# First loads in another order, seven identity products ahead of the first matmul, and later weight loads on ScalarE's queue in a two-layer gated cross-attention kernel

## The chip, the cores and the metric

The kernel runs on one core of a Trainium2 chip. Its time is device microseconds per execution, as the median of several runs. The profile comes from one profiled execution, whose own time stands beside its span below. Engines: PE is TensorE, PEld its weight loads, DVE VectorE, ACT ScalarE, POOL GpSimd, SP SyncE.

## The reference

Two gated layers work on x (8 blocks of 128 rows, 512 wide) and a context of the same shape. Cut to what matters here:

```python
x = x + tanh(g_xattn[0]) * L0_xattn(layernorm(x), ctx, mask, ...)   # 32 heads of 128
x = x + tanh(g_ffn[0])   * L0_ffn(layernorm(x), ...)                # 4-bit weights
x = x + tanh(g_xattn[1]) * L1_xattn(layernorm(x), ctx, ...)         # one head, RMS norms
x = x + tanh(g_ffn[1])   * L1_ffn(layernorm(x), ...)                # base + routed LoRA
# inside L0_xattn:
h_q = (rmsnorm(x) @ w_q.T).reshape(b, lq, 32, 128)
h_k = (ctx @ w_k.T).reshape(b, lk, 32, 128)
h_v = (ctx @ w_v.T).reshape(b, lk, 32, 128)
score = softmax(where(m, h_q·h_k + position_bias, -inf))
out = (score @ h_v) @ w_out.T
```

All of it is float32. The change touches the first stage: the keys h_k and the queries h_q of the first layer's 32 heads, worked on as 16 pairs of heads.

## The kernel before, in words

**Products.** Every float32 operand is split (`split`, lines 163 and 164) into a high part, cast by ScalarE, and a low part, the difference, by VectorE or GpSimd. A product (`product`, lines 172 to 174) is three matmuls: high by high, high by low, low by high.

**The first stage** is `keys_and_queries`. Its list `order` has 32 steps: the keys of pairs 0 to 13, the queries of pairs 0 to 15, the keys of pairs 14 and 15. The first two steps (`PLAIN = 2`) run `project_plainly`: 48 matmuls a pair, from the context blocks B11, B12, B21, B22 (named by the half of the inner dimension and the half of the tokens) and whole weights wk_h, wk_l; ScalarE copies the four results (line 541). All others run `seven`, a scheme of seven block products P1, P5, P6, P2, P7, P4, P3 in that order, 42 matmuls of 128x512 in all. Their results accumulate in PSUM: P1 in c1, P6 on top of it, then P7, then P4. Between them ScalarE copies c1 away: line 237 after P1, 244 after P6, 253 after P7, 259 after P4. TensorE can't write the next product into c1 until the copy of the one before is done; `P5`, and `P2` with the last product of the step before, lie between. VectorE then adds the other terms (lines 248, 254, 263) and SP stores the result to DRAM (line 517).

**Weights.** `load_pair` loads a pair's two weights, 256 KB each, into slots of the tag `raw`, which has six buffers that the sums `more_...` use too; the issue is line 276. A step n loads the pair of step n + 2 first. `pair_sums` makes the sums and differences of the pair of step n + 2 on VectorE (lines 294 to 296; line 306 follows later), and `pair_parts` splits them for step n + 1 (ScalarE casts line 163, low parts line 164 on VectorE, or GpSimd for P1, P2 and P4 in the key steps).

**Operands.** `context_operands` splits the four context blocks (two tiles each, the inner chunk i = 0 or 1) as `cxB..`, and makes the differences T1 to T4 (line 448) as `cxT..`. `query_operands` norms x (line 413 and 414 statistics, 400 roots on GpSimd, 419 on VectorE and 420 on ScalarE for `xq`), transposes it on TensorE by the identity (line 463, tiles `tpx`) and splits the result (469, 473, 484, 488 to 490, 494); in every third step the next part of it begins.

**What sets the order.** TensorE's order in this stage is the program's, fixed by `in_order`. On the other engines a scheduler arranges the instructions by a simulation of its own when the program is built, within their dependencies; each engine then runs its list in order. A DMA that is issued from an engine's queue stands in that engine's list, with the waits for its buffer in front of it. In the kernel before, all loads and stores are issued by SP.

Of the kernel before, what the change touches and what calls it, by code (L numbers as in the profile page):

```python
# [16 lines left out]
P = 128  # L17
NB = 8
D = 512
# [4 lines left out]
HALF = NB // 2  # L24
# [12 lines left out]
}  # L37
LAG = 3
OUT_LAG = 6


def pipeline(starts):
# [18 lines left out]
def kernel(  # L61
# [37 lines left out]
    nc = tc.nc  # L99
# [6 lines left out]
    def keep(shape, name, dtype=F32):  # L106
        return sb.tile(shape, dtype, tag=name, name=name)

    def slot(shape, tag, name, dtype=F32):
        return sb.tile(shape, dtype, tag=tag, name=name, bufs=TAGS[tag])  # L110

    def page(shape, name, dtype=F32R):


        return slot(shape, "page", name, dtype)

    def wide_row(tag, name, dtype=F32):
        return slot([P, D], tag, name, dtype)

    def ptile(shape, tag, name):  # L120
        return psum.tile(shape, F32, tag=tag, name=name, bufs=BANKS[tag])

    def wide(t):

        return t.bitcast(F32)
# [4 lines left out]
    def mark(name, inst):  # L130
        marks[name] = inst.ins
# [30 lines left out]
    def split(high, low, src, low_engine=None):  # L162
        mark("high", nc.scalar.copy(high, src))  # L163
        mark("low", (low_engine or nc.vector).tensor_tensor(low, src, wide(high), ALU.subtract))  # L164
# [16 lines left out]
    HK = NDC // 2  # L181
# [85 lines left out]
    def run(steps):  # L267
        for _ in steps:
            pass
# [1 line left out]

    raws = {}

    def load(key, src, shape=(P, D)):
        t = slot(list(shape), "raw", f"raw_{key}")
        nc.sync.dma_start(out=t, in_=src)
        raws[key] = t

    def load_pair(kind, p):
        if p < NP:  # L280
            w = {"wk": wk, "wq": wq}[kind]
            for h in (2 * p, 2 * p + 1):
                load(f"{kind}_{h}", w[:, h])

    LEFT = ("P1", "P5", "P6", "P2", "P7", "P4", "P3")

# [12 lines left out]
    def pair_parts(kind, p, sums, parts, by_pool=()):  # L299

        for which in LEFT:
            t = parts[which] = slot([P, 2, N], "v", f"{kind}{which}_{p}", F32R)
            with behind("copy"):
                split(t[:, 0], t[:, 1], sums[which], nc.gpsimd if which in by_pool else nc.vector)
            if which == "P2":
                nc.vector.tensor_tensor(sums["P3"], sums["P2"], sums["P6"], ALU.subtract)
            yield
# [53 lines left out]
            biases[g] = t  # L361


    load_pair("wk", 0)
    cx_raw = {}
    for half, dcs in ((0, (0, 1)), (1, (0, 1, 2, 3)), (0, (2, 3))):
        for dc in dcs:
            t = wide_row("wo", f"cxraw{half}{dc}")
            nc.sync.dma_start(out=t, in_=ctxT[:, dc, half * HALF * P : (half + 1) * HALF * P])
            cx_raw[half, dc] = t  # L370
    load_pair("wk", 1)
    lnw = wide_row("pT", "lnw")
    nc.sync.dma_start(out=lnw, in_=ln_w.partition_broadcast(P))
# [9 lines left out]

    ident = keep([P, P], "ident")
    make_identity(nc, ident)
    neghalf = keep([P, NB], "neghalf")
    nc.gpsimd.memset(neghalf, -0.5)

# [34 lines left out]
    def right_pages(name):  # L423
        return {n: page([P, 2, HK, HALF * P], f"{name}{n}") for n in RIGHT.values()}

    def context_operands():

        ops = right_pages("cx")
        ops["B12"] = page([P, 2, HK, HALF * P], "cxB12")
        blocks = {  # L430
            n: [cx_raw.pop((half, 2 * inner + i)) for i in range(HK)]
            for n, half, inner in (("B11", 0, 0), ("B12", 1, 0), ("B21", 0, 1), ("B22", 1, 1))
        }

        def put(n, i, src):
            o = ops[n]
            split(o[:, 0, i, :], o[:, 1, i, :], src, (nc.gpsimd, nc.vector)[i])

        for n, pair in blocks.items():
            for i, t in enumerate(pair):  # L440
                put(n, i, t)
        yield ops
        b11, b12, b21, b22 = blocks.values()
        for n, dst, one, two in (
            ("T1", b11, b12, b11), ("T2", b11, b22, b11), ("T3", b12, b22, b12), ("T4", b21, b21, b11)
        ):
            for i in range(HK):
                nc.vector.tensor_tensor(dst[i], one[i], two[i], ALU.subtract)
                put(n, i, dst[i])
        yield ops  # L450
# [59 lines left out]
    def project(kind, p, left, right):  # L510


        def kept(i, half):
            return slot([P, HALF * P], "kq", f"{kind}{i}{half}_{p}")

        def done(i, half, t):
            nc.sync.dma_start(out=stored[kind, p][:, 2 * i + half], in_=t)

        return seven(f"{kind[0]}{p}", left, right, kept, done)

    def project_plainly(kind, p, left, right):

        banks = {}
        for inner in range(2):
            for half in range(2):
                for i in range(2):
                    if inner == 0:
                        tag = ("mm", "av")[half]
                        banks[i, half] = ptile([P, HALF * P], tag, f"c{i}{half}_{kind[0]}{p}")
                    w, t = left[i], right[f"B{inner + 1}{half + 1}"]  # L530
                    terms = [
                        (
                            tuple(part[:, bass.ts(2 * inner + dc, P)] for part in w),
                            (t[:, 0, dc, :], t[:, 1, dc, :]),
                        )
                        for dc in range(HK)
                    ]
                    product(banks[i, half], terms, inner == 0, inner == 1)
        for (i, half), c in banks.items():
            t = slot([P, HALF * P], "kq", f"{kind}{i}{half}_{p}")  # L540
            mark("copy", nc.scalar.copy(t, c))
            nc.sync.dma_start(out=stored[kind, p][:, 2 * i + half], in_=t)
# [298 lines left out]
    def whole_pair(p):  # L841

        both = []
        for h in range(2 * p, 2 * p + 2):
            high, low = (wide_row("v", f"wk_{n}{h}", F32R) for n in "hl")
            split(high, low, raws.pop(f"wk_{h}"))
            both.append((high, low))
        return both
# [3 lines left out]
    def later():  # L852

        return behind(*(n for n in ("copy", "add") if n in marks))
# [8 lines left out]
    def sums_of(n):  # L863
        if n < len(order):
            k, q = order[n]
            return pair_sums("w" + k[0], q)
# [3 lines left out]
    def keys_and_queries():  # L870
        nonlocal left, sums, before
        for n, (kind, p) in enumerate(order):
            if n + 2 < len(order):
                k, q = order[n + 2]
                load_pair("w" + k[0], q)
            if n < PLAIN:
                if n + 1 == PLAIN:
                    following = {}
                    run(pair_parts("wk", n + 1, sums_of(n + 1), following))
                    sums = sums_of(n + 2)  # L880
                project_plainly(kind, p, left, of_context)
                left = following if n + 1 == PLAIN else whole_pair(p + 1)
                if n == 0:
                    next(making)
                continue
            following, casts = {}, iter(())
            if n + 1 < len(order):
                k, q = order[n + 1]
                casts = pair_parts("w" + k[0], q, sums, following, BY_POOL if n < BEFORE else ())
            now = project(kind, p, left, of_context if kind == "keys" else rows[-1])  # L890
            left = following

            for which in (now, now, before, now, before, now, now):
                next(which, None)
                next(casts, None)
            before = now
            sums = sums_of(n + 2)
            if n == 3:
                with later():
                    prep_mask()  # L900
            if n < BEFORE:
                rows.append(next(of_rows))
            if n in (14, 16, 18, 20):
                with later():
                    residual((n - 14) // 2)
            if n >= BEFORE - 1:
                for _ in range(2 - n % 2):
                    next(extra, None)
        run(before)

    with in_order(*ORD):
        keys_and_queries()
# [30 lines left out]
    def unit(u):  # L943
# [6 lines left out]

        n = 2 * (u - OUT_LAG)

# [322 lines left out]
    def ending():  # L1275

        outs = iter(range(2 * (NU - OUT_LAG), NP * NB))

# [20 lines left out]
    key, ffn, att, last = ([s(b) for b in range(NB)] for s in (keys, ffn0, xattn1, ffn1))  # L1299
# [80 lines left out]
```

## Time and profile before

| what | value |
|---|---|
| median of 3 runs | 959.51 us (958.08 to 962.11) |
| profiled execution | 959.39 us, span 957.6 us, mean granted clock 0.993 |
| TensorE busy | 919.2 us, 96% of the span |
| VectorE, ScalarE, GpSimd busy | 650.3, 505.9, 482.4 us |
| DMA | 175.00 MB, mean 183 GB/s |
| loads of wk and wq | 32 each, 256 KB, 3.6 and 3.9 us from issue to landing |

Busy times are sums over the engine's instructions; the span runs from the first to the last event of the profiled execution, and the rest of its time lies around the span. In a list of waits, a row gives the waiting engine and line, what released it, and the time in total, the number of times and the longest. In a timeline a row gives the start, the duration (of a run of like instructions together), the engine and line, and in brackets the idle time before it and what ended that.

### The profile page before, as it was taken

The numbers are of one execution on the slowest core, as the hardware profiler recorded it, in microseconds if no ns is written. First come the engines' busy times: TensorE is split into PE (matmuls) and PEld (weight loads), VectorE is DVE, ScalarE is ACT, GpSimd is POOL, SyncE is SP. The second block draws the span as 40 slices with busy tenths as digits, with TensorE's granted clock in tenths as the row PEclk, the third lists the DMA queues.
The fourth block names the chain that finished last, engine by engine and source line by source line (L and its number), as shares of the span: only waits on it lengthen the run. The fifth ranks groups of instructions, "written<-read, shape, count | busy, mean of one in ns | idle before, by whom it ended". The sixth has DMA issues, their size and how long they took to land.

```text
span 957.6 us, 16579 instructions
## 1 busy us (share of the span) xinstructions
PE 919.2 (96%) x5444; PEld 807.4 (84%) x5444; DVE 650.3 (68%) x1341; ACT 505.9 (53%) x1435; POOL 482.4 (50%) x524
## 2 busy tenths in 40 slices
PE   6989999999999988999999999999999999899998
PEld 4867788887888788999999999899898997778897
DVE  7777766676678835777766667575666767645686
ACT  5555555665664534454544545354454534666761
POOL 4834323112331485675847658385584852553431
PEclk9999999999999999999999999999999999999999
DMA  9544464789886677677665766566666655513001
GB/s 283 173 145 143 133 216 160 238 259 291 298 265 202 190 233 249 185 205 189 174 200 166 220 183 190 165 180 188 182 192 188 193 166 175 220 61 118 1 24 67
DMA packets 125269, 175.00 MB, mean 183 GB/s; under 512 B 17406, under 2 KB 55294, under 8 KB 124030
## 3 DMA queue, kind: packets, MB, share of 16 engines
q1 hardware_dynamic: 125182, 173.94, 58.2%
q8 instruction: 43, 0.70, 0.3%
q14 instruction: 44, 0.36, 0.2%
HBM read 109.85 MB, written 64.03 MB: 182 GB/s over the span
## 4 chain that ended last, share of the span: by engine, by line
PE 63%; DMA 14%; DVE 11%; issue 4%; POOL 3%; ACT 2%; SPq 2%; DVEq 0%; POOLq 0%; ACTq 0%
PE sc L628 5%; PE pso L174 5%; PE pso L172 5%; PE av L686 5%; PE pso L173 5%; PE c_v L172 4%; PE c_v L173 4%; PE c_v L174 4%; DMA raw_wk<-in_wk_dram 4%; DMA through<-s 4%; PE c_q L172 3%; PE c_q L174 3%; PE c_q L173 3%; DMA moved<-through 2%; PE c_k L172 2%
## 5 line engine op out<-in xcount | busy, mean ns | idle before, releaser
L643 ACT ACTIVATE s<-s,nm 128x128 f32<-128x128 f32 x256 | 99.9, 392 | 123.5 <-DVE nm L633 69.6
L651 POOL TENSOR_TENSOR s<-s,rs 128x512 f32<-128x512 f32 x64 | 66.7, 1043 | 100.0 <-DVE rs L649 64.5
L172 PE MATMUL pso<-wo_h,a 128*128 128x512 f32 x256 | 106.7, 417 | 2.0 <-DVE x L705 2.0
L705 DVE SCALAR_TENSOR_TENSOR x<-pso,tg,x 128x512 f32<-128x512 f32 x128 | 93.8, 734 | 17.6 <-PE pso L174 17.1
L174 PE MATMUL pso<-wo_h,a 128*128 128x512 f32 x256 | 101.7, 397 | 2.0 <-DVE a L688 2.0
L173 PE MATMUL pso<-wo_l,a 128*128 128x512 f32 x256 | 101.9, 398 | 0.0
L616 POOL TENSOR_TENSOR s<-mneg,bias 128x512 f32<-128x512 f32 x64 | 82.5, 1289 | 26.4 <-DMA through<-s 26.4
L172 PE MATMUL c_v<-wvP,cxT 128*128 128x256 f32 x288 | 83.3, 289 | 1.0 <-ACT v L253 0.7
L173 PE MATMUL c_v<-wvP,cxT 128*128 128x256 f32 x288 | 81.8, 284 | 0.0
L174 PE MATMUL c_v<-wvP,cxT 128*128 128x256 f32 x288 | 81.7, 284 | 0.0
L628 PE MATMUL sc<-k,q 128*128 128x128 f32 x512 | 73.4, 276 | 6.2 <-DMA k<-keys 6.2
L671 DVE STREAM_TRANSPOSE pT<-moved 128x512 f32<-128x512 f32 x64 | 45.2, 706 | 46.3 <-DMA moved<-through 46.3
L628 PEld LDWEIGHTS sc<-k,q 128*128 128x128 f32 x512 | 66.8, 192 | 8.5 <-issue 3.5
L688 DVE TENSOR_TENSOR a<-av,a 128x512 fp32r<-128x512 f32 x64 | 43.6, 681 | 44.6 <-ACT a L687 44.4
L686 PE MATMUL av<-pT,v 128*128 128x128 f32 x512 | 68.8, 276 | 5.0 <-DVE pT L671 5.0
L686 PEld LDWEIGHTS av<-pT,v 128*128 128x128 f32 x512 | 63.1, 192 | 6.8 <-DVE pT L671 5.5
L172 PE MATMUL c_v<-wvP,cxB 128*128 128x256 f32 x216 | 62.6, 290 | 0.0
L687 ACT CAST a<-av 128x512 fp32r<-128x512 f32 x64 | 37.3, 583 | 47.8 <-PE av L686 47.7
L164 POOL TENSOR_TENSOR wvP<-raw_wv,wvP 128x512 fp32r<-128x512 f32 x43 | 56.3, 1321 | 11.0 <-ACT wvP L163 11.0
L174 PE MATMUL c_v<-wvP,cxB 128*128 128x256 f32 x216 | 61.6, 285 | 0.0
L173 PE MATMUL c_v<-wvP,cxB 128*128 128x256 f32 x216 | 61.6, 285 | 0.0
L629 DVE TENSOR_TENSOR s<-sc,s 128x512 f32<-128x512 f32 x64 | 44.0, 687 | 23.9 <-PE sc L628 12.1
(276 smaller groups left out, 2801.0 us busy)
## 6 DMA issues: line engine op xcount, KB each, us to landing
keys<-keys SPq DMA_DIRECT2D x64, 256.0 KB, 3.6
queries<-queries SPq DMA_DIRECT2D x64, 256.0 KB, 4.0
q<-queries SPq DMA_DIRECT2D x64, 256.0 KB, 4.2
k<-keys SPq DMA_DIRECT2D x64, 256.0 KB, 4.6
through<-s SPq DMA_DIRECT2D x64, 256.0 KB, 3.7
moved<-through SPq DMA_DIRECT2D x256, 64.0 KB, 2.0
raw_wk<-in_wk_dram SPq DMA_DIRECT2D x32, 256.0 KB, 3.6
raw_wq<-in_wq_dram SPq DMA_DIRECT2D x32, 256.0 KB, 3.9
```

The lines of the kernel that those rows point to most:

```text
L164: mark("low", (low_engine or nc.vector).tensor_tensor(low, src, wide(high), ALU.subtract))
L172: nc.tensor.matmul(out, lhsT=lh, rhs=rh, start=first, stop=False, **more)
L173: nc.tensor.matmul(out, lhsT=lh, rhs=rl, start=False, stop=False, **more)
L174: nc.tensor.matmul(out, lhsT=ll, rhs=rh, start=False, stop=last, **more)
L616: nc.gpsimd.tensor_tensor(s, mneg[:, half], bias.unsqueeze(2).to_broadcast([P, NQ, HALF, Q32]), ALU.add)
L628: nc.tensor.matmul(ps[:, j, :], lhsT=q[:, cols], rhs=k[:, cols], start=True, stop=True)
L629: nc.vector.tensor_tensor(s, by_block(ps), s, ALU.add)
L643: e = nc.scalar.activation(one, one, AF.Exp, bias=nm[:, j : j + 1], accum_out=sm[:, j : j + 1])
L651: mark(f"norm{u}", nc.gpsimd.tensor_tensor(s, s, factors, ALU.mult))
L671: nc.vector.transpose(by_block(t), probs[u])
L686: nc.tensor.matmul(av[:, b, :], lhsT=v[:, cols], rhs=pT[:, b, :], start=True, stop=True)
L705: "x", nc.vector.scalar_tensor_tensor(xs[b], ps, factor, xs[b], ALU.mult, ALU.add, **out)
```

## The change

There are four edits.

1. The first loads on SP's queue are issued in the order wk_0, cx00, cx01, wk_1, cx10, cx11, cx02, cx03, cx12, cx13 instead of wk_0, wk_1, cx00, cx01, cx10, cx11, cx12, cx13, cx02, cx03 (the first digit is the half of the tokens, the second the inner chunk). wk_2 and wk_3 follow in both.
2. After the identity is made, TensorE multiplies it by itself seven times into a PSUM tile that nothing reads.
3. The low part of the first tile of block B11 is made by VectorE instead of GpSimd.
4. In the steps of `keys_and_queries` the weights of the pair of step n + 2 are loaded from ScalarE's queue instead of SP's: 60 loads in all.

```diff
+WARMING = 7
...
-    def load(key, src, shape=(P, D)):
+    def load(key, src, shape=(P, D), queue=nc.sync):
         t = slot(list(shape), "raw", f"raw_{key}")
-        nc.sync.dma_start(out=t, in_=src)
+        queue.dma_start(out=t, in_=src)
         raws[key] = t
 
-    def load_pair(kind, p):
+    def load_pair(kind, p, queue=nc.sync):
         if p < NP:
             w = {"wk": wk, "wq": wq}[kind]
             for h in (2 * p, 2 * p + 1):
-                load(f"{kind}_{h}", w[:, h])
+                load(f"{kind}_{h}", w[:, h], queue=queue)
...
-    load_pair("wk", 0)
     cx_raw = {}
-    for half, dcs in ((0, (0, 1)), (1, (0, 1, 2, 3)), (0, (2, 3))):
-        for dc in dcs:
-            t = wide_row("wo", f"cxraw{half}{dc}")
-            nc.sync.dma_start(out=t, in_=ctxT[:, dc, half * HALF * P : (half + 1) * HALF * P])
-            cx_raw[half, dc] = t
+    for inner in range(2):
+        for half in range(2):
+            if inner == 0:
+                load(f"wk_{half}", wk[:, half])
+            for dc in range(inner * HK, inner * HK + HK):
+                t = wide_row("wo", f"cxraw{half}{dc}")
+                nc.sync.dma_start(out=t, in_=ctxT[:, dc, half * HALF * P : (half + 1) * HALF * P])
+                cx_raw[half, dc] = t
     load_pair("wk", 1)
...
     make_identity(nc, ident)
+
+    idle = ptile([P, P], "av", "idle")
+    for _ in range(WARMING):
+        nc.tensor.matmul(idle, lhsT=ident, rhs=ident, start=True, stop=True)
...
-            split(o[:, 0, i, :], o[:, 1, i, :], src, (nc.gpsimd, nc.vector)[i])
+            by_pool = i == 0 and n != "B11"
+            split(o[:, 0, i, :], o[:, 1, i, :], src, nc.gpsimd if by_pool else nc.vector)
...
-                load_pair("w" + k[0], q)
+                load_pair("w" + k[0], q, nc.scalar)
```

TensorE's list is the same but for the seven products. ScalarE's list has the loads between its casts and copies, and the scheduler has arranged the lists of ScalarE, VectorE and GpSimd differently in the first 60 us and in a few steps near 225 us.

## The prediction

> **What bounds the kernel now.** I read the page's busy shares first, then the chain, then the waits of TensorE, then a table by stage, and last the timelines of ScalarE, VectorE and TensorE at the places that the change touches.
>
> ```profile
> PE 919.2 (96%) x5444; PEld 807.4 (84%) x5444; DVE 650.3 (68%) x1341; ACT 505.9 (53%) x1435; POOL 482.4 (50%) x524
> PE c_k L172 <- ACT cxB L163: 6.8, 1, 6.8
> PE c_k L172 <- ACT keys L244: 5.1, 3, 3.4
> PE c_q L172 <- ACT queries L237: 1.8, 1, 1.8
> PE c_k L173 <- DVE cxB L164: 1.3, 1, 1.3
> ```
>
> TensorE is busy 96% of the span and its order is written out, so only its idle time can be won. In the stage that the change touches (keys and queries, 0 to about 325 us) that is: 6.8 us before the first matmul, 0.6 and 1.3 at the start, 5.1 in three waits for a copy of keys (3.38, 0.85, 0.85) and 1.8 for a copy of queries. All but the first few are waits for ScalarE's copies, and ScalarE was late because of others.
>
> ```profile
> 10.00:15.00 5.00, 5.00 (x17) 3.96 (x16) 5.00 (x4) 4.10 (x8) 4.09 (x4) 1.00 1.06 396
> 15.00:20.00 5.00, 3.73 (x17) 2.75 (x16) 5.00 (x8) 1.27 (x3) 1.39 (x1) 1.00 1.07 285
> 20.00:25.00 5.00, 5.00 (x24) 4.14 (x23) 5.00 (x10) 3.83 (x9) 3.13 (x2) 1.00 0.90 264
> 30.00:35.00 5.00, 5.00 (x24) 4.14 (x23) 5.00 (x20) 4.30 (x10) 4.75 (x7) 1.00 0.14 54
> ```
>
> The columns after the width are busy time of TensorE, its weight loads, VectorE, ScalarE and GpSimd, the granted clock, the DMA share and GB/s. VectorE is busy 5.00 of 5.00 in every slice from 10 to 35 us: it paces the start, and the DMA engines are full from 10 to 20.
>
> ```profile
> 35.85 0.60 ACT L237 COPY keys<-c_k 128x512 f32<-128x512 f32 x1
> 36.50 0.50 PE L172 MATMUL c_k<-cxT,wkP 128*128 128x512 f32 x1
> 53.20 0.58 ACT L244 COPY keys<-c_k 128x512 f32<-128x512 f32 x1
> 53.84 0.56 PE L172 MATMUL c_k<-cxT,wkP 128*128 128x512 f32 x1 [3.38 <-ACT keys L244]
> ```
>
> The copy of step 2's first product ends at 36.45 and the third product, which writes over it, starts at 36.50: no slack is left there. The second pair is the large stall; after it the matmuls come every 0.427 us until 57.58 instead of every 0.2275 (nine of them, 1.8 us), and the granted clock is 0.75 in 55 to 60. So this stall costs 3.4 + 1.8 = 5.2 us.
>
> **The start.** SP issues one load every 0.43 us; the first, third and fourth landed by 3.43, 6.12 and 7.60 (starts of the casts that waited), the second before 4.06. Context block 00 moves from third to second, 01 from fourth to third. Its cast (0.62) then ends between 4.7 and 6.7; I take 5.3, which is nearer the second load's row. The low part now comes from VectorE (0.69) behind the first wk_l (to 4.75): the second matmul at 6.0 (5.4 to 7.5) instead of 8.15. VectorE's unbroken run, which began at 8.26, can start by 1.5 us earlier (01 at 6.12 for 7.60), and carries 0.69 more, so it is 0.8 us ahead (0 to 1.5). GpSimd loses the 1.27 us low part, which nobody waits for any more. The matmul that waits for VectorE at 18.20 then starts at about 17.4 (16.7 to 18.2).
>
> The seven products of the identity: the nearest rows are the transposes by the identity, 0.27 us each. Between 0.27 and twice that they last 1.9 to 3.8 us, from the identity (ready at 1.33) to 3.2 to 5.1: before any operand lands, so they cost nothing; if they overran they would delay the first matmul by at most 0.4. What they can raise is the clock: thirteen matmuls ran at 0.427 until 13.00, worth 13 x 0.2 = 2.6 us. But the wait that follows at 18.20 is for VectorE: a faster TensorE only waits longer there. I count 0 for the clock.
>
> The Trainium skill, "TensorE: Matmul & The Clock Gate", Part 1, speaks against the products: full clock comes only after about one window of 3.4 us of sustained activity, and the window is free-running. Here 6.2 us passed from the first matmul to the full pace, so row and rule differ; by the rule seven products and a gap may not lift the clock, by the row they don't, and either way the sum stays.
>
> **Step 2.** ScalarE now issues the loads of later pairs, in order with its copies. In the built order the first load of pair 4 stands after two of the four copies of pair 1, behind a wait for VectorE's last low part of pair 2's P4 to free its buffer; then come a copy, two xq scalings, a copy, a cast, the second load, and only then the copy of step 2's first product. At SP's 0.38 an issue and ScalarE's rows that is 0.38 + 0.58 + 2 x 0.72 + 0.58 + 0.39 + 0.38 + 0.60 = 4.4 us after VectorE. Before, VectorE did that low part by 35.92. In the new order about 3.7 us of its work (two xq, two statistics, the aggregates, L306) stand behind it, 0.7 new ahead, and it begins 0.8 earlier: 32.1, up to 35 if GpSimd's tensor work slows it as it does elsewhere. The copy ends at 36.5 to 39.4; I take 37.0. So step 2's third product starts 0.5 us later than before (0 to +2.9), and the start's gain is gone: it has become a wait of about 2 us there, up to 5.
>
> **The stall at 53.84.** Behind it stood VectorE's L294, which waited 2.70 us for a raw_wk load with the transposes' chain (L489, L490) queued behind it. The new order puts that chain ahead of L294: 2.7 us won. But two L419 (2.35 us beside GpSimd) and two xq scalings (0.72 each) now stand ahead of the copy that TensorE waits for: 1.5 to 3.1 lost. Net -1.2 to +0.4 for that product; I take +0.4, since GpSimd was at work in this stretch. As TensorE then comes 0.5 later, the stall is about 3.3, or split over several copies. Its cold clock (1.8) may go or stay: I take half, -0.9; and a new wait at step 2 could bring one more (+1.8 at most).
>
> **The later steps.** 52 of the 60 moved loads fall in 60 to 300 us, where ScalarE is busy 139.2 of 240. 60 x 0.38 = 23 us of issue go onto it, in the gap that it has before L253 in each step (2 us and more). TensorE needs that copy 12 matmuls x 0.2275 = 2.7 us later, so a copy may be 2.1 us late unseen. SP's queue loses the same 60 and its slot waits, and the stores L517 leave sooner; nobody waits for those. The waits of 0.85 near 86 and 116 stand behind xq scalings and stay: 0 (down to -1.7). The 1.83 at 229.97 came from ScalarE's L566 waiting for VectorE's L564; around there the order changes, and I take it as gone: -1.8 (0 to -1.8). The page's transition to the attention units waits for DMA and GpSimd, which the change leaves alone: 0.
>
> On queues, the Trainium skill's "Trainium Kernel Development and Optimization", Key Constraints, says that issuing from several engines saves only issue time, the 16 DMA engines being the same. The trace agrees that bandwidth isn't what is bought; by that rule the move is worth at most SP's 23 us of issue, none of it on the path.
>
> **Sum.** Against the profiled run, span 957.6 and 959.4 with the 1.8 around it: step 2 and the 53.84 stall +0.4, cold clock -0.9, queries' wait -1.8, ScalarE's issues +1.0 (0 to +2: a few copies late by one 0.38): -1.3, so 958.1. The median is 0.1 above the profiled run: 958.2.
>
> **The rivals.** (A) *The stalls go.* The 53.84 stall vanishes with its cold clock (5.2), and 0.85 x 2 and 1.83 too: 959.5 - 8.7 = 950.8. For it: the L294 wait was its proximate cause. Against: ScalarE's queue gains waits at the same copies, and its L237 in step 2 has no slack now. (B) *ScalarE is held at its loads: slower.* Each load waits for its raw buffer; SP's L276 waited for VectorE and GpSimd 26.5 + 23.4 + 5.5 + 4.8 + 0.5 = 60.7 us in 25 waits. If these pass to ScalarE, and the part of each over the 2.1 us slack reaches TensorE, that is 60.7 - 25 x 2.1 = 8.2 us: 967.7. It decides if a buffer comes free later than 2.1 us after ScalarE is ready for L253. Against it: in step n = 5 the two buffers were free at 65.58 and 65.30, and L253 ran at 66.63 only. In the query steps the second comes free near 167.5 where L253 ran at 166.95: 1.0 late, within the slack. (C) *The products don't raise the clock*: nothing lost, by the wait at 18.20; within the forecast.
>
> **How the numbers follow.** What can be told from no change is about 0.5%, 4.8 us: 954.7 to 964.3. My case (start's gain swallowed, small gains after) gets 0.58; its own bounds are -1.2 - 1.8 - 1.8 = -4.8 below (954.7) and 2.9 + 2.0 = +4.9 above (964.4, the old cold clock and the queries' wait kept). (A) gets 0.22 and (B) 0.20, each with half its weight beyond its price. The range from 951 to 967.5 leaves out some 0.2. I choose 958.2.
>
> **What would show it.** Right: the first matmul near 5.5, the wait at 18.20 still for VectorE, then a wait of some 2 us for L237 near 35, a smaller or split stall near 53, no wait at 230, and ScalarE's loads in its gaps. Wrong: TensorE ahead by 1 us or more at 60 us (A), or a repeated wait for L237, L253 or L259 in steps between 60 and 300 us with ScalarE's queue stopped at a load (B).

## The result and the profile after

| | before | after |
|---|---|---|
| median of 20 runs | 959.97 us (955.55 to 966.23) | 960.89 us (954.26 to 965.00) |
| ratio to before | | 1.0007, 95% interval 0.9986 to 1.0029 |
| profiled execution | 959.39 us, span 957.6 | 963.92 us, span 962.1 |

No change that can be measured. The forecast was 958.2 us with "within 0.5%" the likeliest. Single executions of one kernel lie 10 us apart, so the traces below, one execution each, are read for places and waits, and the medians for the sum. Line numbers moved: lines 163, 172, 237 and 276 of before are 164, 173, 238 and 277 here, lines 420 and 541 are 427 and 549.

The waits of TensorE for keys and queries (c_k and c_q; line, what released it, us in total, times, longest):

```profile
PE c_k L173 <- ACT keys L238: 3.7, 3, 2.7
PE c_k L173 <- ACT cxB L164: 1.5, 2, 1.0
PE c_k L173 <- ACT keys L245: 1.5, 3, 0.8
PE c_q L173 <- ACT queries L238: 1.2, 3, 0.5
PE c_k L173 <- ACT keys L254: 1.1, 1, 1.1
PE c_k L174 <- DVE cxB L165: 0.4, 1, 0.4
```

The 3.4 us stall and the 1.8 us for the queries' copy are gone, and the first matmul starts 1.5 us earlier (the products fill most of the time ahead of it). In their place ScalarE's copies are late in other steps. TensorE's timeline of the same kernel shows where (in the first row each of the seven products counts as two instructions):

```profile
1.39 3.35 PE L392 MATMUL idle<-ident 128*128 128x128 f32 x14 [1.39 <-POOL ident masks.py:199]
5.31 0.80 PE L173 MATMUL c_k<-cxB,wk_h 128*128 128x512 f32 x1 [0.57 <-ACT cxB L164]
8.21 0.79 PE L173 MATMUL c_k<-cxB,wk_h 128*128 128x512 f32 x1 [0.95 <-ACT cxB L164]
17.04 0.50 PE L174 MATMUL c_k<-cxB,wk_h 128*128 128x512 f32 x1 [0.38 <-DVE cxB L165]
38.17 0.50 PE L173 MATMUL c_k<-cxT,wkP 128*128 128x512 f32 x1 [2.68 <-ACT keys L238]
57.61 0.50 PE L173 MATMUL c_k<-cxT,wkP 128*128 128x512 f32 x1 [1.13 <-ACT keys L254]
84.81 0.50 PE L173 MATMUL c_k<-cxT,wkP 128*128 128x512 f32 x1 [0.84 <-ACT keys L245]
```

TensorE started 1.5 us earlier and had the 29th matmul 1.2 us earlier (17.04 for 18.20). At step 2 it waited 2.7 us where it had not waited before, and was 1.7 us late there (38.17 for 36.50). Why the copy came so late is in ScalarE's list at that place:

```profile
34.08 0.34 ACTq L277 DMA_DIRECT2D raw_wk<-in_wk_dram  x1
34.52 0.59 ACT L549 COPY keys<-c_k 128x512 f32<-128x512 f32 x1 [3.84 <-DVE stats L421]
36.13 0.72 ACT L427 ACTIVATE xq<-xq,stats 128x512 f32<-128x512 f32 x1 [0.41 <-DVE stats L421]
36.55 0.33 ACTq L277 DMA_DIRECT2D raw_wk<-in_wk_dram  x1
37.53 0.59 ACT L238 COPY keys<-c_k 128x512 f32<-128x512 f32 x1
```

ScalarE stood 3.84 us at a load whose buffer VectorE had not yet freed (its last low part of pair 2 ran to 34.05), and the copy that TensorE needed stood behind it, with six instructions between. (The row names L421, VectorE's next event; the low part is what the load waits for in the built order.) In the kernel before that copy began at 35.85. From there the stall of 53.84 is replaced by 0.16, 1.13 and 0.36, too short in this execution for the half clock, so that at step 5 the changed kernel leads by 0.9 us and at step 20 by 1.7.

Then the loads hold ScalarE again, now in the query steps:

```profile
268.79 1.03 ACT L164 CAST wqP<-raw_wq 128x256 fp32r<-128x256 f32 x3
273.62 1.61 ACTq L277 DMA_DIRECT2D raw_wq<-in_wq_dram  x2
275.27 0.59 ACT L254 COPY queries<-c_q 128x512 f32<-128x512 f32 x1 [5.45 <-DVE wqP L165]
```

```profile
246.83 0.50 PE L173 MATMUL c_q<-xqT,wqP 128*128 128x512 f32 x1 [0.52 <-ACT queries L238]
266.55 0.50 PE L173 MATMUL c_q<-xqT,wqP 128*128 128x512 f32 x1 [0.39 <-ACT queries L238]
275.91 0.50 PE L173 MATMUL c_q<-xqT,wqP 128*128 128x512 f32 x1 [0.86 <-ACT queries L254]
277.83 0.50 PE L173 MATMUL c_q<-xqT,wqP 128*128 128x512 f32 x1 [0.27 <-ACT queries L238]
```

As I read the lists, here is a ring: the load is issued late, so VectorE's sums are late, so the low part that frees the buffer is late, so the next load is late, and ScalarE's copies stand behind it. The first fence shows ScalarE idle 5.45 us, the second the four waits of TensorE, 2.0 us in all. They cost more than that, since the first matmul behind a wait takes longer to its successor (0.34 us for 0.23 at 275.91) and shorter waits come with them: the matmul at 232.14 before starts at 228.74 here, and the one at 300.14 at 300.85. So this stretch took 72.1 us for 68.0, 4.1 more, where the lost wait at 229.97 had won 1.7.

At 345 us, the end of the stage, the changed kernel's trace led by 0.1 us, at 606 us by 1.4; by the first output add (line 1241 of before) it was 4.5 us behind. No edit touches that part, but the lists do differ: the built order moves instructions of ScalarE and GpSimd in the second layer too (the first at 836.9 us of before, the last at 851.2), which the description of the change above left out. Two questions, then: what each edit is worth, and where the lead goes.

### The profile page after: what moved, and what is told of

Read it like the earlier page. It is cut to its first block, busy times and chain, and to the rows that moved or that the text cites. A ratio compares the mean times of both kernels' runs of the same rounds, so it can differ in the third digit from the quotient of the medians.

```text
span 962.1 us, 16602 instructions
## 1 busy us (share of the span) xinstructions
PE 928.0 (96%) x5458; PEld 811.0 (84%) x5458; DVE 652.3 (68%) x1342; ACT 504.3 (52%) x1435; POOL 478.7 (50%) x523
## 4 chain that ended last, share of the span: by engine, by line
PE 47%; DMA 5%; DVE 3%; SPq 2%; ACT 2%; POOL 1%; issue 1%; DVEq 0%; POOLq 0%; ACTq 0%
PE pso L173 5%; PE pso L175 5%; PE pso L174 5%; PE av L694 5%; PE sc L636 4%; PE c_v L174 4%; PE c_v L173 4%; PE c_v L175 4%; DMA through<-s 3%; DMA moved<-through 2%; SPq L671 1%; PE o L173 1%; PE tph L1017 1%; PE psq L173 1%; PE psq L175 1%
## 5 line engine op out<-in xcount | busy, mean ns | idle before, releaser
L659 POOL TENSOR_TENSOR s<-s,rs 128x512 f32<-128x512 f32 x64 | 66.7, 1042 | 100.9 <-DVE rs L657 72.2
L175 PEld LDWEIGHTS pso<-wo_h,a 128*128 128x128 f32 x256 | 48.7, 190 | 13.5 <-DVE a L696 2.4
```

What stands on the lines that cost most here:

```text
L175: nc.tensor.matmul(out, lhsT=ll, rhs=rh, start=False, stop=last, **more)
L659: mark(f"norm{u}", nc.gpsimd.tensor_tensor(s, s, factors, ALU.mult))
```

## The experiments

My theory was that the start is worth a little, that ScalarE's loads take it back at step 2 and again after 240 us, and that the products are worth nothing. The rivals: VectorE paces the start, so nothing is won at all; or the loads are what gains.

**E1, the first three edits alone.**

```diff
-                load_pair("w" + k[0], q, nc.scalar)
+                load_pair("w" + k[0], q)
```

> The first three edits alone; every weight load stays on SP's queue. Theory (the start is worth a little, and ScalarE's loads gave it back in step 2): first matmul at 5.3, the copy of step 2's first product (37.53 in the changed kernel, 35.85 before) at 34.5 to 35.9, no 2.7 us wait of TensorE there; the stall near 53 stays near 3 us as in the kernel before, since no load has left VectorE's wait; the first product's copy at step 20 (214.23 changed, 215.94 before) at 214 to 216; whole time within 3 us of before. Rival (VectorE paces the start, so nothing is won at all): the copy of step 2 at 35.9 or later and step 20 at 216.

Measured: 961.98 us where before was 959.72 (as for E2 to E4), 1.0019 (0.9999 to 1.0040). TensorE's three longest waits after the start, in its trace:

```profile
35.58 0.50 PE L173 MATMUL c_k<-cxT,wkP 128*128 128x512 f32 x1 [1.59 <-ACT keys L238]
52.65 0.50 PE L173 MATMUL c_k<-cxT,wkP 128*128 128x512 f32 x1 [3.06 <-ACT keys L245]
228.85 0.78 PE L173 MATMUL c_q<-xqT,wqP 128*128 128x512 f32 x1 [2.04 <-ACT queries L238]
```

The 29th matmul came at 14.91, step 2's copy at 34.93 (0.9 us before that of before), the stall near 53 stayed, and step 5 led by 2.8 us: 1.8 of it is the half clock, which did not come this time behind 3.06 us of idling (the end of this document says why). So the start does win something in this trace, but the median doesn't show it. The wait at step 2 is not the loads' alone: 1.6 us of it stay here and in E3, E10 and E12, where SP issues the first loads, since TensorE comes to it earlier than the copy can; what goes is the lateness of the copy.

**E2, the fourth edit alone,** on the kernel before (with the `queue` argument of the diff above):

```diff
-                load_pair("w" + k[0], q)
+                load_pair("w" + k[0], q, nc.scalar)
```

> The fourth edit alone: start as before, loads of later pairs on ScalarE's queue. Theory: a wait of TensorE for the copy of step 2's first product of 1 to 4 us, the copy at 38 or later (35.85 before); the 3.4 us stall near 53 smaller than 2; then the waits for ScalarE's copies around 245 to 280 as in the changed kernel (2 us in four waits), with ScalarE stopped for 3 to 5 us ahead of its loads in steps 22 to 24; step 20's copy 0 to 2 us later than in the changed kernel (214 to 216). Rival (the gain of the changed kernel at 60 to 270 us comes from the start): step 20's copy at 216 or later.

Measured: 962.09 us, 1.0030 (1.0007 to 1.0052): slower by 0.3%. Step 2's copy at 38.48, TensorE's wait there 2.24, then 1.92 at 46.77 for GpSimd; the large stall gone; step 20 at 218.10, 2.2 us later than before. Of the waits after 240 two remain, 0.88 and 0.26. On the old start ScalarE's loads alone cost; they pay for the lost stall with the waits at steps 2 and 3.

**E3, ScalarE's loads from step 3 on.**

```diff
-                load_pair("w" + k[0], q, nc.scalar)
+                load_pair("w" + k[0], q, nc.scalar if n >= 3 else nc.sync)
```

> The changed kernel, but the loads of steps 0 to 2 go back to SP's queue; ScalarE issues from step 3 on. Theory: the 2.7 us wait for step 2's copy is gone or under 1 us, so TensorE is 1 to 3 us ahead of the changed kernel at 60 us; from there as the changed kernel, with the waits at 245 to 280. Whole time 1 to 3 us under the changed kernel. Rival (the wait at step 2 is VectorE's work, whoever issues the loads): the copy of step 2 still at 37 and nothing won.

Measured: 961.52 us, 1.0019 (0.9994 to 1.0043). The 29th matmul at 15.38, step 2's copy at 35.44, the wait 1.61 where under 1 was expected, and no stall above 0.9 near 53; step 5 at 66.44, 0.6 ahead of the changed kernel, not 1 to 3. Where the first loads stay on SP the 29th matmul was at 14.9 to 15.4 (E1, E3, E12 below), where ScalarE issues them at 16.5 to 17.2 (after, E4, E5, E7, E8, E11); but E10, on SP, had 16.59, as its block 01 landed late. So the order of ScalarE's list is worth perhaps 1 to 2 us there, and the whole did not gain by it.

**E4, no products.**

```diff
-WARMING = 7
+WARMING = 0
```

> The changed kernel without the seven identity products. Theory: the full matmul pace begins some 0 to 3 us later than the 12.5 of the changed kernel, TensorE waits less for VectorE at the 29th matmul, and from that matmul on (17.04) all is the same within 0.3 us: the products are worth nothing. Rival (the products' clock is worth up to 13 x 0.2 = 2.6 us): the 29th matmul 1 us or more later.

Measured: 958.83 us, 0.9986 (0.9967 to 1.0005). Full pace from 14.2 us instead of 12.5, the 29th matmul at 16.78 instead of 17.04: as the theory has it, the clock is worth nothing there. But the median is 2 us lower, which neither theory had, and the two traces did not stay within 0.3 us: at step 31's first copy E4 led by 3.0 us. It has none of the four waits between 240 and 280 us, with the same loads on ScalarE. Nor are the products the only difference: in the built order of E4 and of E7 below, one of ScalarE's copies (line 549) stands ahead of step 2's second load, and TensorE waited 2.2 us there instead of 2.7.

**E5 and E6, the order of the last section.** After tracing, ordering edges pin ScalarE's and GpSimd's lists in the second layer, in E5 to those of the kernel before, in E6 (on the kernel before) to those of the changed kernel. `LATE` holds the two permutations:

```diff
+    late_from = len(nc.cur_bb.bb.instructions)
     with in_order(*ORD):
         pipeline(starts)
+    for engine, ranks in LATE.items():
+        traced = [i for i in nc.cur_bb.bb.instructions[late_from:] if i.engine == engine]
+        for one, two in zip(ranks, ranks[1:]):
+            tc.add_manual_dep(traced[two], traced[one].name, ...)
```

> The changed kernel, with the lists of ScalarE and GpSimd in the last section (second layer, from about 800 us) pinned to the order that the kernel before has there; the edits of the start alter that order by the scheduler's simulation, though no code there is touched. Theory (the start's 1.4 us at 640 us are lost again in that section): 958 to 959.5 us, 1.5 to 3 us under the changed kernel, and TensorE's wait for the first h1T copy is smaller. Rival (the late difference is chance from one execution to the next): within 1 us of the changed kernel's 960.9.

> The kernel before, with only the lists of ScalarE and GpSimd in the last section pinned to the order of the changed kernel. Theory (that order costs): 1.5 to 3.5 us above before. Rival (chance): within 1 us of before; up to 640 us the trace is that of before within 1 us either way.

Measured: E5 960.30 us where before was 961.78, 0.9987 (0.9962 to 1.0012), against 1.0007 of the changed kernel; E6 962.05, 1.0015 (0.9988 to 1.0041). Both go the way of the theory, by 2.0 and 1.5 parts in a thousand, and neither interval excludes chance. The expected smaller wait for h1T did not come: it is 2.65 us in E5 and 1.95 in the changed kernel. E6's trace was not within 1 us of that of before up to 640 us: with the same lists up to 836.9 us it was over 2 us behind at 606 and 5.4 at 830. So a lead of a few us between two traces can be chance alone.

**E7, no products, last section as before.** The products, their tile with them, are taken out, and the section pinned as in E5.

> The changed kernel without the identity products, and with the last section in the order of the kernel before: a candidate. Theory: as the run without products, less the late loss: 956 to 958 us, the stage of keys and queries ends 0 to 3 us earlier than before's 345.4. Rival (late order is chance): 958 to 960.

Measured: 956.92 us where before was 961.78, 0.9947 (0.9925 to 0.9969). This one is faster than both kernels, by about half a percent.

```profile
5.08 0.79 PE L173 MATMUL c_k<-cxB,wk_h 128*128 128x512 f32 x1 [5.08 <-ACT cxB L164]
16.45 0.50 PE L174 MATMUL c_k<-cxB,wk_h 128*128 128x512 f32 x1 [0.39 <-DVE cxB L165]
37.09 0.50 PE L173 MATMUL c_k<-cxT,wkP 128*128 128x512 f32 x1 [2.20 <-ACT keys L238]
57.11 0.50 PE L173 MATMUL c_k<-cxT,wkP 128*128 128x512 f32 x1 [1.18 <-ACT keys L254]
246.55 0.50 PE L173 MATMUL c_q<-xqT,wqP 128*128 128x512 f32 x1 [0.87 <-ACT queries L238]
```

TensorE's timeline has much the same waits as the changed kernel's at steps 2 to 4, but one between 240 and 280 us where that had four.

**E8, ScalarE's loads in steps 0 to 19 only,** with the products, pinned as in E5:

```diff
-                load_pair("w" + k[0], q, nc.scalar)
+                load_pair("w" + k[0], q, nc.scalar if n < 20 else nc.sync)
```

> The changed kernel with ScalarE's loads only in steps 0 to 19 and SP's afterwards, the last section in the order of the kernel before. Theory (ScalarE is held at its loads in the query steps, where its copies then come late): the four waits between 245 and 280 us, 2.0 us in all, are gone; in exchange the wait of 1.8 us near 228, which the kernel before has, comes back, perhaps with a half clock behind it (the run of the start alone lost 2.0 and 1.6 there); ends the stage within 1 us of the changed kernel; 957.5 to 960. Rival (those waits are chance): they stay.

Measured: 959.51 us where before was 961.78, 0.9985 (0.9956 to 1.0014). The four waits between 240 and 280 are gone, and 1.83 at 226.83 is back, the same wait as in the kernel before. So the waits after 240 come with the loads, and moving the loads trades one for the other. In all fourteen traces the wait near 230 is 1.8 us or more where SP issues the loads of those steps and under 0.9 where ScalarE does; waits between 240 and 280 us come in six of the seven kernels where ScalarE does, not in E4. The trade is not even: the stage ended 3.6 us ahead of the changed kernel's, not within 1 us. The start of this execution also answers for the products: full pace came with the third matmul, at 6.09, and TensorE then waited for its operands instead,

```profile
8.65 0.50 PE L173 MATMUL c_k<-cxB,wk_h 128*128 128x512 f32 x1 [0.88 <-ACT wk_h L164]
13.35 0.50 PE L174 MATMUL c_k<-cxB,wk_h 128*128 128x512 f32 x1 [1.27 <-DVE cxB L165]
16.75 0.50 PE L174 MATMUL c_k<-cxB,wk_h 128*128 128x512 f32 x1 [0.34 <-DVE cxB L165]
```

so that the 29th matmul, the last of these rows, was no earlier than in E4 (16.78), which reached full pace at 14.2.

**E9, the products alone,** on the kernel before, whose other lists stay as they were:

```diff
     make_identity(nc, ident)
+
+    idle = ptile([P, P], "av", "idle")
+    for _ in range(7):
+        nc.tensor.matmul(idle, lhsT=ident, rhs=ident, start=True, stop=True)
```

> The kernel before with the seven identity products alone; every other engine's list is that of before. Theory (the products are worth nothing, since VectorE sets the 29th matmul): full matmul pace up to 2 us sooner than the 13.0 of before, the 29th matmul within 0.5 us of 18.20, the whole within 1 us of before. Rival (the products cost 2 to 4 us, as the two pairs of runs with and without them suggest: 960.9 and 958.8, 960.3 and 956.9): 962 to 965 where before is 960.

Measured: 963.77 us where before was 961.72, 1.0020 (0.9993 to 1.0046). The median lies with the rival, though the interval includes no change. At the start TensorE waited for the other engines:

```profile
6.13 0.50 PE L172 MATMUL c_k<-cxB,wk_h 128*128 128x512 f32 x1 [1.40 <-ACT cxB L163]
7.48 0.50 PE L173 MATMUL c_k<-cxB,wk_h 128*128 128x512 f32 x1 [0.85 <-POOL cxB L164]
17.36 0.50 PE L173 MATMUL c_k<-cxB,wk_h 128*128 128x512 f32 x1 [1.86 <-DVE cxB L164]
```

The wait for VectorE is 1.86 where before had 1.27: the clock's gain is waited away. Behind it the matmuls fell back to 0.43 us apart (granted clock 0.50 from 18.24 to 21.65 us), so that TensorE, 0.8 us ahead at the 29th matmul, was 0.8 behind at 30 us; the next waits took that up again (0.6 ahead at 53.84). The 29th matmul at 17.36 is no gain either, since E6, whose start is that of before without products, has it at 17.51.

**E10, E11 and E12, without products, the last section as before,** with no loads on ScalarE, with those of steps 0 to 19, and with those from step 3 on.

> The first and third edits alone (load order, low part on VectorE), no products, loads on SP's queue, last section in the order of the kernel before. Theory: as the run of the start alone: 2 to 3 us ahead of before at 60 us, ahead by 1 to 3 at the stage's end if no half clock comes behind the wait near 228, else 0; whole 957 to 960 where before is 960. Rival (the gain over before comes from ScalarE's loads): 960 or more.

> No products, ScalarE's loads in steps 0 to 19 only, last section in the order of the kernel before: the other candidate. Theory: as the best run so far (0.995 of before), within 1.5 us, the 1.8 us wait near 227 back and the waits at 245 to 280 gone. Rival (what is won comes from the loads after step 20): 0.998 or more.

> No products, ScalarE's loads from step 3 on, last section in the order of the kernel before. Theory (the loads of the first three steps cost ScalarE its casts): matmul 29 near 15.4 instead of 16.5, step 2's copy 1 to 2 us sooner than in the changed kernel (37.5), the whole within 1 us of the run with all loads on ScalarE. Rival (those loads are what removes the stall near 53): a wait of 2 us or more near 53.

Measured, where before was 961.72: E10 957.89 us, 0.9957 (0.9930 to 0.9984); E11 957.90, 0.9965 (0.9946 to 0.9984); E12 959.04, 0.9972 (0.9950 to 0.9995). In E10, the first and third edits alone, the stall near 53 is 2.60, with the half pace behind it, and that near 230 is 1.80: both stay, the trace leads by 0.4 us at 60 us and not by 2 to 3, and the median is still as low as E7's, within the intervals. In E11 the waits after 240 are gone and 2.04 at 228.30 is back. In E12 the 29th matmul came at 14.98, step 2's copy at 35.00, and no wait near 53 was over 0.73; the whole was 2.5 parts in a thousand above E7, not within 1 us.

The five kernels with the new load order and the products, and the five without, sorted by the last section's order (ratios to before, the mean of those in a cell):

| | last section as changed | last section as before |
|---|---|---|
| products | 1.0015 (after, E1, E3) | 0.9986 (E5, E8) |
| no products | 0.9986 (E4) | 0.9960 (E7, E10, E11, E12) |

Both steps are 2.6 to 2.9 parts in a thousand, some 2.5 us, in both rows and both columns, while where the loads are issued moves a cell's members by 2.5 parts at most (E7 to E12), within one interval. Each single ratio is uncertain by 2 to 3 parts. E6 (+1.5) and E9 (+2.0) on the kernel before agree in sign. E1 to E4, E5 to E8 and E9 to E12 were measured on three different chips, each with the kernel before beside them; so the step between the columns is also one between chips, and E6 alone tests the order beside before on one chip. The products are tested most closely by E5 against E7, on one chip.

The traces speak against the order of the last section as the cause of its step. From unit 54's scores (line 629) to the first output add, the nine executions with the old last section took 193.1 us on average (189.8 to 195.5) and the five with the new one 195.1 (193.3 to 196.1). But 1.6 of these 2.0 us lie ahead of the first instruction that the order moves; behind it, from the transposes at 837 us on, the two groups took 88.1 us (86.5 to 89.6) and 88.5 (87.1 to 90.0). So 0.5 us can be the order's, and the rest of the step between the columns is chance or the chip.

Of the products, nothing is to be seen until step 20: 214.3 on average with, 214.2 without; at step 31's first copy 326.1 with and 324.0 without, with a scatter of 2 us in each group. Where ScalarE issues the later loads, this lies in the stretch of the four waits: the matmuls that take 68.0 us before (from 232 to 300 us) took 71.6 to 72.2 with products (after, E3, E5) and 68.5 to 70.4 without (E4, E7, E12). The granted clock, averaged over each kernel's runs, is 0.9929 (after) and 0.9933 (E5) with products and 0.9950 (E4) and 0.9952 (E7) without; 0.002 of 958 us is 1.9 us (an estimate), so much of the cost may be time at half pace. On the kernel before it is not so (E9 0.9927, before 0.9926). I found no mechanism that joins products of 1.4 to 4.7 us to a delay after 214 us. E4 keeps the products' PSUM tile, and so the turn that it takes in that tag's three buffers, and is still faster than the changed kernel; so the tile seems not to be it. I leave the products' cost as measured and unexplained, and a cost of the last section's order as not shown.

## Why the prediction was right, and where not

The range held and no change was the likeliest case, but that the sum of -1.3 us is near the trace's -1.4 at 606 us is luck. At the end of the stage, 345 us, TensorE led by 0.1 only, terms that were off having cancelled; the rest came between 345 and 400 us, where the kernel before had two stretches at half pace (from 354.5 and 368.2) and the changed kernel one (from 353.9). The prediction's own signs also came on both sides: those of its case, and with them TensorE 1.2 to 1.9 us ahead near 60 us, its sign of (A), and repeated waits after 240 us, its sign of (B). By steps:

- **First matmul.** Near 5.5 forecast, 5.31 measured, the second at 6.04 against 6.0. Not foreseen: block 01's load landed only at 7.54 in this execution (5.71 in E1), so VectorE was not 0.8 ahead but 0.1 (8.19 for 8.26). The 29th matmul at 17.04, forecast 17.4.
- **The products' clock at 0.** Right at the start, in both directions (E4, E9). That they could cost was in no term: I priced only an overrun of 0.4. They ended at 4.74, inside the bounds. The Trainium skill's rule ("TensorE: Matmul & The Clock Gate", Part 1, "What's actually happening") that full clock needs a window of about 3.4 us of activity, and that the window is free-running, agrees with the scatter: with products the full pace began between 6.1 (E8) and 14.4 us (E5), without between 8.9 (E12) and 14.2 (E4, E2). My "6.2 us" don't differ from it, as I had said: by the clock's windows at the end of this document they are one from 6.35 to 9.76 us with 1.00 us of idle time in it and one without any, to 13.18.
- **Step 2.** The mechanism held: a start's gain that becomes a wait (1.6 us without the loads), and a copy of line 237 that is late behind ScalarE's loads; 2.7 us, forecast some 2. Its size was off: the product came at 38.17, not at 37.0. The term that failed is VectorE's release, 32.1 taken and 34.05 measured, 35 being the upper bound; the 4.4 us of ScalarE behind it were 4.1.
- **The stall at 53.84.** I took it to stay near 3.3 and half of its cold clock to go. It fell to 1.65 in three waits with no cold clock. L489 and L490 ahead of the load's wait seem to have been worth more than the two xq scalings cost; no run tests that alone. From step 2 to step 5 TensorE went from 1.7 behind to 0.9 ahead, -2.6 where my terms gave -1.0 (from +0.5 to -0.5), and that made up for step 2.
- **Later steps.** The 1.83 near 230 went as forecast. ScalarE's issues, at +1.0 (0 to +2), were mis-sized: 4.1 us in the stretch from 232 to 300 us alone. Rival (B)'s mechanism was there, but TensorE paid in four steps and not in 25 waits, half of the price of 8.2 us; the slack hid the rest. (The rows behind that price left out one of the same list, three waits for `wkP L164`, 7.8 us; with it, it is 9.7.)
- **What was in no term.** A cost of the products beyond their own length, and what the traces lose after 606 us; the last section's order, which no edit touches, can be 0.5 us of that.
- **Rival (A)** supposed that all stalls go, 950.8. The large one and the 1.83 did go in this trace, one of the 0.85 stayed (0.84 at 84.81) and the other became 0.48; but others came. E7 with 0.9947 is the nearest to it, and it needs the products out.

On queues, the rule of "Trainium Kernel Development and Optimization", Key Constraints, that issuing from several engines saves only issue time, agrees with E10 against E7: 0.9957 with all loads on SP, 0.9947 with 60 of them on ScalarE, within the intervals. What the move buys and costs here is the order of waits on the engine that issues.

## What to carry to other kernels

A DMA in a compute engine's queue brings its buffer wait with it: before moving loads there, find what frees their buffers and what stands behind them on that engine, and leave them on an idle queue where the buffer comes free late. An earlier start is worth nothing until the next step that paces has been found (here VectorE at the 29th matmul and ScalarE's copy at step 2). And with a scheduler that orders a whole program, compare the built lists to the end of it: an edit at 5 us moved instructions at 837 us. Before such a move is blamed, see whether the time is lost behind the first moved instruction; here most of it was lost ahead of it.

## What was not expected of the hardware

Whether TensorE falls back to half pace after a wait isn't told by the wait's length, but by where the wait lies. In each of the fourteen traces the granted clock changes only at whole multiples of 3.413 us from its first change (in the kernel before at 13.18, 54.14, 57.55, 354.51 us and so on), and it stays at a half for one such window or two. The first lines are of the kernel before, the second of E9: a window with the larger part of a wait of 1.83 us in it, and the window behind it (the first number after the width is TensorE's busy time as the profile models it, the third from the end the granted clock).

```profile
228.22:231.63 3.41, 1.66 (x7) 1.40 (x8) 1.93 (x7) 3.41 (x8) 0.00 (x0) 1.00 0.96 351
231.63:235.04 3.41, 3.41 (x16) 2.83 (x16) 3.38 (x7) 1.61 (x5) 1.44 (x1) 1.00 0.89 264
```

```profile
226.45:229.86 3.41, 1.58 (x8) 1.00 (x7) 1.99 (x9) 2.38 (x5) 0.03 (x1) 1.00 0.90 330
229.87:233.28 3.41, 3.41 (x10) 2.63 (x9) 3.34 (x7) 2.60 (x7) 1.36 (x1) 0.50 0.63 197
```

In the kernel before, 0.08 us of the wait fall into the window ahead, and this one has 1.75 us idle; in E9 all 1.83 us lie in one window, and half pace follows. Over all traces 52 windows at full clock were followed by one at half, each with 1.72 us idle or more; of the 3775 that were not, none had more than 1.88. So the same wait of 1.83 us brought about eight matmuls at 0.43 us in E9 and in E6, and none in the kernel before and in E8; 2.04 us brought them in E1 and not in E11, where it lay in two windows with 1.03 and 1.02. Near 53 us, 3.38 (before), 3.73 (E6) and 2.60 (E10) brought the half pace, and 2.75 (E9) and 3.06 (E1) did not. Each time it cost 1.6 to 1.8 us.

At the start it is the same grid: in E8 the products fill the window from 1.49 to 4.90 us but for 0.17 us, and the full clock comes at 4.90; in the changed kernel the window from 2.30 to 5.71 has 0.57 us idle, and it comes at 12.54. The Trainium skill ("TensorE: Matmul & The Clock Gate", Part 1) puts the fall back behind an idle window of about 3.4 us. The width of the window agrees; but here about half of it idle was enough, so the measurement decides. Since the windows lie elsewhere in each execution (the first change at 13.18 us in the kernel before, 12.54 in the changed kernel, 10.46 in E1), a stall of 2 to 3 us has to be priced with a chance of the half pace. It is a part of what a single execution of this kernel scatters: the profiled ones had two to six such windows after the start, at 1.7 us each 3.4 to 10 us (an estimate), and E3's, with two, was still the slowest but one of its kernel's twelve runs at 968.08 us.
